# Loading the dense batches' expert weights once, into retired row buffers, with shorter packed rows

## The chip, the cores and the metric

The kernel runs on one core of a Trainium2 chip. The core has TensorE (PE, with its weight loads PEld), VectorE (DVE), ScalarE (ACT), GpSimd (POOL) and SyncE (SP); SP, ACT and POOL issue DMAs, which 16 DMA engines carry out. The metric is the device time of one execution in microseconds (us); of several runs the median is taken.

## What is computed

The input `x` has 64 batches of 256 rows of 256 float32 values. Two layers follow each other, each with attention over a graph and then a feed-forward part:

```
x = x + gnn0(layernorm(x), adj)              # 4 heads of 64, ELU at the end
x = x + (layernorm(x) @ weight.T + bias)
x = x + gnn1(layernorm(x), adj)              # 1 head of 256, ReLU at the end
x = x + moe(layernorm(x))
# gnn: q = h @ W; e = leaky_relu(q.a_src + q.a_dst), masked by adj; softmax(e) @ q
# moe: tokens t (16384 of them); probs = softmax(t @ router.T); the 2 best of 8 experts,
#      their weights made to sum to 1:
#      out = t + sum over the two e of weight_e * (gelu(t @ w1[e] + b1[e]) @ w2[e] + b2[e])
```

All of it is in float32. Which two experts a row goes to is known only on the chip.

## The kernel before

**Stages.** A generator `batch_layers` takes one batch through both attention layers, the feed-forward layer and the last norm. It leaves the normed rows in a tile `xe` of the ring tagged `xng`, which has `XNG` = 8 buffers of 128 partitions x 2 rows x 260 values (256 of the row and 4 of routing data). The mixture of experts is done in one of two ways:

- *Routed*, batches 0 to 60. `route` works in chunks of 4, 2 or 1 batches. It works out where each row goes and sends rows with indirect DMAs on POOL (`send`, L1066) from `xe` to a DRAM buffer `xs`, which is sorted by expert. `expert_pair` then works on 256 rows of one expert. On SP it loads the rows (`xr`, four DMAs at L906, in a ring of 5 buffers), their routing data (`xt`, L917, 14 buffers) and the expert's first weights (`we`, L935, a ring of `WBUFS` = 7 buffers). The rows are transposed on DVE (L117), `hidden` multiplies by the first weights (L968) and applies GELU (L974), `result` multiplies by the second weights (L983) and adds the bias (L993), ACT scales by the row's weight (L961). `scatter` (L1004) then adds the 256 rows to the output with two indirect DMAs on POOL. There are 129 pairs; the last 14 (`FLUSH`) are filled up with spare rows that are written at L1170.
- *Dense*, batches 61 to 63. `dense_expert` applies every expert to all rows of a batch and adds the result, weighted, to a tile `base` (L1036), which `store_dense` (L1047) stores at the end on SP. The batches are in two groups, {61} and {62, 63}; for each group each of the 8 experts is one job. Each of these 16 jobs loads the expert's first weights itself (L1026), into the same `we` ring that the routed pairs use. Second weights and biases (`w2s`, `b2s`) stay in SBUF for the whole kernel.

**Packed weights.** `pack_expert` writes each expert's first weights and bias into a DRAM tile `wpack[e]` of 128 rows of `WROW` values: 512 weights, from `C_B1` = 512 on two bias values, then zeros. `WROW` is 576 before, so a row has 2304 bytes.

**Order of the work.** The loop at the end writes the order out by hand, in steps, three (`TICKS`) for each new batch. Each job is a generator. What it yields is its rank in the next step (or, if negative, a rank in the same step); within a step jobs go on in the order of rank. The instructions of each engine, and of each DMA queue, run in the order thus written. In the step in which the job of expert 0 for batch 61 issues its load (at rank 90), batch 63 makes its `xe` tile (at rank 29); in the steps after it, one dense load and the loads of one pair follow each other on SP until all eight experts of the first group are loaded. `dense_free` spaces the jobs of the second group two steps apart.

**Waits.** A tile taken from a ring waits until all that used the buffer's last holder is done. A scatter waits until the two scatters of the pair before have landed (`added[-2:]`, L1001).

Of the kernel before, what the change touches and what calls it, by code (L numbers as in the profile page):

```python
# [9 lines left out]
F32 = mybir.dt.float32  # L10
# [5 lines left out]
P = 128  # L16
# [11 lines left out]
def kernel(  # L28
# [17 lines left out]
    nc = tc.nc  # L46
    B, N, D = x.shape
# [3 lines left out]
    KT = D // P  # L51
    NT = N // P
# [16 lines left out]
    ROW = D + 4  # L69
# [3 lines left out]
    io = ctx.enter_context(tc.tile_pool(name="io", bufs=2))  # L73
    work = ctx.enter_context(tc.tile_pool(name="work", bufs=2))
    small = ctx.enter_context(tc.tile_pool(name="small", bufs=4))
    keep = ctx.enter_context(tc.tile_pool(name="keep", bufs=1))
# [194 lines left out]

    C_B1, WROW = KT * D, KT * D + 64
    WBUFS, XBUFS, YBUFS = 7, 5, 9
    wpack = tc.dram_tile([E, P, WROW], F32, name="wpack")
    w2s = const.tile([P, E, KT * D], F32, tag="w2s", name="w2s")
# [41 lines left out]
    def once(work):  # L319
# [14 lines left out]
        out=tri, in_=tri, pattern=[[1, P]], base=0, channel_multiplier=-1,  # L334
# [157 lines left out]
    for i in range(2):  # L492
        t = keep.tile([P, NT, D + 1], F32, tag=f"q1_{i}", name=f"q1_{i}")
# [260 lines left out]
            dense_batch[b] = dict(base=base, xT=xT)  # L754

    XNG = 8
    dense_batch = {}

    def dense_home(b):

# [203 lines left out]
    def hidden(xT, we):  # L964
        ph = bank("ph", [KT, PAIR])
        for f in range(KT):
            for k in range(KT):
                nc.tensor.matmul(  # L968
                    ph[:, f, :], we[:, k * D + f * P : k * D + (f + 1) * P], xT[:, k, :],
                    start=(k == 0), stop=(k == KT - 1),  # L970
                )
        hT = work.tile([P, KT, PAIR], F32, tag="hT", name="hT", bufs=5)
        for f in range(KT):
            nc.scalar.activation(  # L974
                hT[:, f, :], ph[:, f, :], AF.Gelu, bias=we[:, C_B1 + f : C_B1 + f + 1]
            )
        return hT

    def product(hT, e):
        py = bank("py", [2, D])  # L980
        for t in range(2):
            for f in range(KT):
                nc.tensor.matmul(  # L983
                    py[:, t, :], hT[:, f, t * P : (t + 1) * P],
                    w2s[:, e, f * D : (f + 1) * D].rearrange("p e c -> p (e c)"),
                    start=(f == 0), stop=(f == KT - 1),
                )
        return py
# [33 lines left out]
    def dense_expert(e, group):  # L1022

        yield 90
        we = io.tile([P, WROW], F32, tag="we", name="we", bufs=WBUFS)
        nc.sync.dma_start(out=we, in_=wpack[e])  # L1026
        yield 40
        for b in group:
            own = dense_batch[b]
            yield 35  # L1030
            hT = hidden(own["xT"], we)
            yield -85
            py = product(hT, slice(e, e + 1))
            for t in range(NT):
                for add in (py[:, t, :], b2s[:, e, :]):
                    nc.vector.scalar_tensor_tensor(  # L1036
                        own["base"][:, t, :], add, own["w"][:, t, e : e + 1],
                        own["base"][:, t, :], op0=ALU.mult, op1=ALU.add,
                    )
            if e == E - 1:  # L1040
                begin(store_dense(b), 99)

    def store_dense(b):

        own = dense_batch[b]
        yield 99
        d = nc.sync.dma_start(  # L1047
            out=out_rows[b * N : (b + 1) * N, :].rearrange("(t p) d -> p t d", p=P),
            in_=own["base"],
        )  # L1050
        tc.declare_no_dep(d.ins, query=SYNC, group="out", reason="no row is added to here")
        tc.add_to_no_dep_group("out", d.ins)
        nc.sync.nop()
# [6 lines left out]
    def begin(job, rank):  # L1060
        active.append([rank, len(order), job])
        order.append(job)
# [126 lines left out]
    def route_dense(b, lg):  # L1189

        c = len(CHUNKS) + 1 + b - ROUTED
        ohs, ed = in_one(top_two(c, NT, lg, chunk_tile([NT], "first", c)))
        yield 75
        two = chunk_tile([2, NT], "two", c)
        nc.scalar.activation(two[:, 0], ed, AF.Tanh, scale=-0.5)
        second_weight(two[:, 1], two[:, 0])
        nc.vector.tensor_tensor(two[:, 0], two[:, 0], two[:, 1], ALU.add)
        w = chunk_tile([NT, E], "wd", c, DENSE)
        nc.vector.tensor_tensor(
            ohs, ohs, two[:, :, :, None].to_broadcast([P, 2, NT, E]), ALU.mult  # L1200
        )
        nc.vector.tensor_tensor(w, ohs[:, 0], ohs[:, 1], ALU.add)
        dense_batch[b]["w"] = w
        for group in GROUPS:
            if b == group[-1]:
                dense_jobs.extend(
                    (len(group), lambda e=e, g=group: dense_expert(e, g)) for e in range(E)
                )
# [109 lines left out]
```

## Time and profile before

| | |
|---|---|
| median of 3 runs | 1486.39 us (1485.40 to 1491.55) |
| profiled execution, its own time | 1489.83 us |
| its span, first to last instruction | 1488.0 us |
| mean granted TensorE clock | 0.985 |
| TensorE busy | 1420.1 us, 95% |
| VectorE, ScalarE, GpSimd busy | 83%, 68%, 58% |
| loads of first weights | 145, of 288 KB each |
| loads of rows `xr` | 516, of 64 KB each |
| scatters | 258 |
| DMA traffic | 236.10 MB, mean 159 GB/s |

The profile page gives busy time by engine, then the span in 40 equal slices with the busy share of each in tenths, then the chain of work that ended last, and the groups of instructions. Timelines list instructions of one engine: start, duration, engine, line, operation, tiles; in brackets is the idle time before it and what ended that, as far as the trace shows it. A DMA that SP issues is shown with the time of its issue[...]. The records of single packets give their queue, size, start and duration. Lists of waits give the engine and line, what it waited for, the sum in us, how often, and the longest.

### The profile page before, as it was taken

Reading aid. Unit: us, or ns where it says so; the run is one execution under the profiler, and the core shown is the slowest. Engines: PE = TensorE matmul, PEld = TensorE weight load, DVE = VectorE, ACT = ScalarE, POOL = GpSimd, SP = SyncE. Lnnn points to the kernel's source line nnn. Section 1 sums busy time; section 2 is a strip of 40 time slices with the busy share of each in tenths; the row PEclk is TensorE's granted clock in tenths of the full one; section 3 lists DMA queues with packets and bytes.
Section 4 is the critical chain, followed back from the end, with each engine's and each line's share of the span. In section 5 each row is a group of like instructions: output and inputs, shape, how many; then the busy total and the mean of one; then the engine's idle time right before and its main releaser. Section 6 shows DMA issues by size and latency. Waiting matters only on the chain. (4 is left out here: it accounts for less than half of the span.)

```text
span 1488.0 us, 29865 instructions
## 1 busy us (share of the span) xinstructions
PE 1420.1 (95%) x8138; PEld 1264.0 (85%) x8138; DVE 1232.9 (83%) x4320; ACT 1006.5 (68%) x2389; POOL 864.6 (58%) x851
## 2 busy tenths in 40 slices
PE   6899999999999999999999999999999999899994
PEld 5688888898999999899999989888888888778883
DVE  7689999988898889899888989998888888765442
ACT  1377667577777777777777787777777878643330
POOL 2122446455857676666758585776666668544444
PEclk9899999999999999999999999999999999999998
DMA  4832243567878777787877687768877786988743
GB/s 128 227 98 86 89 130 117 146 172 153 199 171 193 161 177 170 171 185 180 190 156 190 147 193 168 190 164 186 193 158 172 153 173 128 213 201 150 152 66 49
DMA packets 354081, 236.10 MB, mean 159 GB/s; under 512 B 246260, under 2 KB 316156, under 8 KB 353916
## 3 DMA queue, kind: packets, MB, share of 16 engines
q1 hardware_dynamic: 301000, 157.90, 42.1%
q0 software_dynamic: 48864, 66.33, 23.9%
q10 hardware_dynamic: 4052, 9.98, 2.3%
q8 instruction: 67, 1.10, 0.3%
q14 instruction: 98, 0.80, 0.2%
HBM read 146.00 MB, written 88.09 MB: 157 GB/s over the span
## 5 line engine op out<-in xcount | busy, mean ns | idle before, releaser
L1004 POOL DMA_INDIRECT out_dram<-y,xt x258 | 415.6, 1611 | 214.6 <-issue 54.6
L584 PE MATMUL pv<-q,z 128*128 128x65 f32 (+1 forms) x2560 | 363.7, 297 | 0.7 <-DVE z L570 0.3
L584 PEld LDWEIGHTS pv<-q,z 128*128 128x128 f32 x2560 | 331.2, 193 | 13.3 <-DVE z L570 1.3
L1066 POOL DMA_INDIRECT xs<-xng,pos x244 | 256.3, 1050 | 65.2 <-issue 57.7
L983 PE MATMUL py<-w2s,hT 128*128 (+1 forms) x1224 | 282.9, 382 | 4.7 <-ACT hT L974 4.5
L983 PEld LDWEIGHTS py<-w2s,hT 128*128 128x128 f32 x1224 | 229.7, 191 | 37.2 <-ACT hT L974 7.4
L570 DVE SCALAR_TENSOR_TENSOR z<-z,q,mask 128x256 f32<-128x256 f32 x504 | 231.5, 482 | 15.5 <-DMA z<-terms 6.5
L968 PE MATMUL ph<-sT,we 128*128 128x256 f32 x1032 | 241.4, 383 | 1.6 <-DVE sT L117 0.9
L968 PEld LDWEIGHTS ph<-sT,we 128*128 128x128 f32 x1032 | 195.6, 192 | 28.7 <-DVE sT L117 1.4
L961 ACT ACTIVATE y<-y,w 128x256 f32<-128x256 f32 x258 | 113.4, 499 | 119.4 <-DVE y L993 119.2
L459 ACT COPY xT<-pt 128x512 f32<-128x512 f32 x209 | 121.2, 588 | 82.1 <-PE pt L453 80.0
L974 ACT ACTIVATE hT<-ph,we 128x256 f32<-128x256 f32 x306 | 124.1, 472 | 64.1 <-PE ph L968 46.7
L406 POOL TENSOR_SCALAR rstd<-mv 128x4 f32<-128x4 f32 (+1 forms) x66 | 15.9, 240 | 224.8 <-DVE mv L379 175.3
L504 PE MATMUL pq<-wx,xT 128*128 128x259 f32 x512 | 126.5, 390 | 13.9 <-ACT xT L459 13.9
L424 ACT ACTIVATE off<-x,sums 128x256 f32<-128x256 f32 x256 | 129.2, 505 | 9.2 <-DVE x L667 3.3
L993 DVE TENSOR_TENSOR y<-py,b2s 128x512 f32<-128x512 f32 x129 | 86.9, 687 | 56.3 <-PE py L983 44.8
L469 PE MATMUL pq<-wx,xT 128*128 128x268 f32 x512 | 128.1, 394 | 2.4 <-DVE xT L117 1.2
L504 PEld LDWEIGHTS pq<-wx,xT 128*128 128x128 f32 x512 | 96.0, 192 | 33.6 <-ACT xT L459 19.8
L660 PE MATMUL pf<-wfT,xT 128*128 128x256 f32 x512 | 124.2, 386 | 0.0
L469 PEld LDWEIGHTS pq<-wx,xT 128*128 128x128 f32 x512 | 97.9, 192 | 21.7 <-DVE xT L117 1.4
L688 ACT ACTIVATE rel<-pv,rinv 128x256 f32<-128x256 f32 x128 | 54.0, 469 | 82.1 <-DVE rinv L591 81.8
L660 PEld LDWEIGHTS pf<-wfT,xT 128*128 128x128 f32 x512 | 94.9, 196 | 10.6
(170 smaller groups left out, 2355.7 us busy)
## 6 DMA issues: line engine op xcount, KB each, us to landing
we<-wpack SPq DMA_DIRECT2D x145, 288.0 KB
xr<-xs SPq DMA_DIRECT2D x516, 64.0 KB
z<-terms SPq DMA_DIRECT2D x46, 512.0 KB
xin<-in_x_dram SPq DMA_DIRECT2D x64, 256.0 KB
out_dram<-base SPq DMA_DIRECT2D x61, 256.0 KB
xblk<-in_x_dram SPq DMA_DIRECT2D x188, 64.0 KB
z<-terms ACTq DMA_DIRECT2D x17, 512.0 KB
out_dram<-y,xt POOLq DMA_INDIRECT x258
```

Source lines behind the costliest of these rows:

```text
L424: nc.scalar.activation(off, src[:, t, :], AF.Square, bias=sums[:, t : t + 1], scale=-float(D), accum_out=sq[:, at + t : at + t + 1],)
L459: nc.scalar.copy(dst, pt)
L469: nc.tensor.matmul(pq.rearrange("p h c -> p (h c)"), xT[:, k, t * P : (t + 1) * P], wx[:, k, :], start=(k == 0), stop=(k == KT - 1),)
L504: nc.tensor.matmul(pq, xT[:, k, t * P : (t + 1) * P], wx1[:, k, :], start=(k == 0), stop=(k == KT - 1),)
L570: nc.vector.scalar_tensor_tensor(z[:, j, :, h, :], terms, q[:, j, h, HD + 2 : HD + 3], masks[0][:, j, :].rearrange("p (t i) -> p t i", t=N ...
L584: nc.tensor.matmul(pv[:, h, :], z(j, h, t), q[:, j, h, : d + 1], start=(j == 0), stop=(j == NT - 1),)
L660: nc.tensor.matmul(pf[:, t, :], xT[:, k, t * P : (t + 1) * P], wfT[:, k, :], start=(k == 0), stop=(k == KT - 1),)
L968: nc.tensor.matmul(ph[:, f, :], we[:, k * D + f * P : k * D + (f + 1) * P], xT[:, k, :], start=(k == 0), stop=(k == KT - 1),)
L974: nc.scalar.activation(hT[:, f, :], ph[:, f, :], AF.Gelu, bias=we[:, C_B1 + f : C_B1 + f + 1])
L983: nc.tensor.matmul(py[:, t, :], hT[:, f, t * P : (t + 1) * P], w2s[:, e, f * D : (f + 1) * D].rearrange("p e c -> p (e c)"), start=(f == 0 ...
L1004: d = nc.gpsimd.indirect_dma_start(out=out_rows, out_offset=bass.IndirectOffsetOnAxis(ap=xt[:, t, 0:1].bitcast(I32), axis=0), in_=y[:, t, ...
L1066: d = nc.gpsimd.indirect_dma_start(out=xs_d[: E * CAP * PAIR, :], out_offset=bass.IndirectOffsetOnAxis(ap=at, axis=0), in_=xe, in_offset=None,
```

## The change

- A packed row has 512 + 16 values, 2112 bytes, rather than 2304. This holds for the packing, and for the routed pairs' loads.
- A dense job loads its expert's first weights only if no dense job has loaded them before. The tile comes from the ring `xng` of normed rows rather than from `we`, and holds 514 values (2056 bytes) in each partition. The tiles are kept in a dictionary `dense_weights`, so the second group's jobs find the first group's.

No other instruction is added, removed or moved in the written order.

```
-    C_B1, WROW = KT * D, KT * D + 64
+    C_B1, WROW = KT * D, KT * D + 16
...
-    dense_batch = {}
+    dense_batch, dense_weights = {}, {}
...
     def dense_expert(e, group):
 
         yield 90
-        we = io.tile([P, WROW], F32, tag="we", name="we", bufs=WBUFS)
-        nc.sync.dma_start(out=we, in_=wpack[e])
+        if e not in dense_weights:
+            we = keep.tile([P, NT, ROW], F32, tag="xng", name=f"wd_{e}", bufs=XNG)
+            we = we.rearrange("p t c -> p (t c)")[:, : C_B1 + KT]
+            nc.sync.dma_start(out=we, in_=wpack[e, :, : C_B1 + KT])
+            dense_weights[e] = we
+        we = dense_weights[e]
         yield 40
         for b in group:
             own = dense_batch[b]
```

## The prediction, made before the changed kernel had run

> **What bounds the kernel now.** I read the page first for the balance of the engines, then the chain that ended last in order of time, then the timelines of POOL and SP over the last 180 us, where the change acts. The page says that one engine is nearly full:
>
> ```profile
> span 1488.0 us, 29865 instructions
> PE 1420.1 (95%) x8138; PEld 1264.0 (85%) x8138; DVE 1232.9 (83%) x4320; ACT 1006.5 (68%) x2389; POOL 864.6 (58%) x851
> PE   6899999999999999999999999999999999899994
> DMA  4832243567878777787877687768877786988743
> ```
>
> From slice 2 to slice 39 TensorE is at 80% or more, nearly always at 90%; the DMA engines are at 60 to 90%. In most of the span a transfer that comes sooner gains nothing. The end is different. The chain in order of time, its last 55 us:
>
> ```profile
> 1432.13 3.45 PE py L983 x16
> 1435.58 3.47 PE ph L968 x16
> 1439.22 0.28 issue
> 1439.51 0.48 ACT hT L974
> 1440.01 3.77 DMA out_dram<-y,xt
> 1443.91 0.71 issue
> 1444.62 1.56 POOL out_dram L1004
> ...
> 1478.34 1.56 POOL out_dram L1004
> 1479.89 1.86 POOLq L1313
> ```
>
> The last thing to end is not TensorE (its last matmul starts at 1467.28) but the scatters of L1004: two per pair of 256 rows, and each pair's scatter waits until the one before has landed. The chain view hands over to TensorE at 1439, but the trace shows that this is not where the scatters begin to set the pace. The last pair's rows `y` are weighted at 1447.67 and scattered from 1478.34, 31 us later; a pair at 1347 is already 25 us behind its `y`, and from 1317 on none is under 15 us. So over the whole tail the scatters run one behind the other. POOL's timeline gives the time of a step (first scatter of a pair to the first of the next):
>
> ```profile
> 1309.86 1.61 POOL L1004 DMA_INDIRECT out_dram<-y,xt  x1 [1.55 <-DMA out_dram<-y,xt]
> ...
> 1346.98 1.56 POOL L1004 DMA_INDIRECT out_dram<-y,xt  x1 [4.04 <-DMA xr<-xs]
> ...
> 1355.23 1.56 POOL L1004 DMA_INDIRECT out_dram<-y,xt  x1 [4.83 <-DMA xr<-xs]
> ...
> 1406.30 1.56 POOL L1004 DMA_INDIRECT out_dram<-y,xt  x1 [4.00 <-DMA xr<-xs]
> ...
> 1464.02 1.56 POOL L1004 DMA_INDIRECT out_dram<-y,xt  x1 [3.04 <-ACT hT L974]
> ```
>
> From 1406.30 to 1464.02 there are 9 steps: 6.41 us each. From 1309.86 to 1406.30 there are 13: 7.42 us each, 8.25 in the worst (1346.98 to 1355.23). The 13 steps are 96.44 - 13 x 6.41 = 13.1 us longer than undisturbed ones. These 13.1 us are all that the change can reach on the path that sets the end. By the packet records of those steps: the packets of a scattered pair take 3.0 to 3.2 us where nothing else moves; beside weights and rows they take up to 4.7. Over the 25 last steps this window is fitted, within 0.11 us, by 3.09 + 0.62 x (engine time of weight packets inside it) + 0.35 x (of rows `xr` and `xt`) + 0.58 x (of a store). The weights have 11.8 us inside the 13 windows, so 7.3 us of the 13.1; rows 9.3 us, so 3.3; one store 0.4; the remaining 2.1 is a later start of five of the windows.
>
> **Part 1: eight loads less.** SP's timeline, and what SP waited for in this tail:
>
> ```profile
> 1341.52 0.35 SPq L935 DMA_DIRECT2D we<-wpack  x1
> 1343.30 0.35 SPq L1026 DMA_DIRECT2D we<-wpack  x1
> 1343.88 1.94 SPq L906 DMA_DIRECT2D xr<-xs  x4
> ...
> SPq L1026 <- PE ph L968: 28.1, 12, 5.7
> ```
>
> L1026 is a dense load, L935 a routed one. Sixteen dense loads become eight: those of the second group (issued at 1357.11, 1369.14, 1382.96, 1396.77 and four from 1410.58 to 1424.40) go. The last four lie behind 1406.30, where their packets (from 1.0 to 2.5 us after issue) miss the scatter windows: no gain. Between 1309.86 and 1406.30 there are 27 weight loads (16 routed, 11 dense); 4 go. Taking the 7.3 us as spread evenly, 23/27 of it stays, 6.2 us: a gain of 1.1. The bounds: 0.3 us, because by their time of issue only the one of 1357.11 overlaps a window (0.85 us of weights in that step, at most half of it this load's, x 0.62), and 3.0 us, from comparing the six steps with one pair and one dense load each (1.15 us above 6.41) with the later seven that have fewer dense loads (0.88); solved for two unknowns, this gives 0.34 a pair and 0.75 a dense load, which hangs on the phases. I take 1.1.
>
> Here a rule bears. The Trainium skill ("DMA: Bandwidth & Descriptors", section "Queues, rings and completion order") says that a DMA engine takes turns between the queues that have work, a packet at a time. By it a microsecond of weights in a window would cost up to a whole microsecond, 11.8 in place of 7.3, and part 1 would give 1.7. The fit to the windows says 0.62; I use the fit.
>
> **Part 2: rows of 2112 bytes.** A routed load keeps its 128 packets, each 2112 bytes instead of 2304; a dense one has 2056. In the records a packet of 2304 bytes takes 93 ns in the median and one of 2080 bytes 85 ns, so 2112 should take 86: a load's engine time goes from 128 x 93/16 = 744 to 688 ns. A page speaks against this edit: by the skill (same page, section "How a descriptor splits into AXI transactions") reads go in 32-byte beats from 256-byte boundaries, and bytes ahead of an unaligned start are fetched too. 2304 is nine times 256, so with an aligned start every row is 72 beats; 2112 leaves three rows of four off the boundary, 69 beats on average rather than 66, hence 89 ns instead of 86. The row of 2080-byte packets is nearer, though these are stores into the row buffer and not reads from it; the two differ by 24 ns a load. On 6.2 us it gives 8% (by the rule 4%): 0.5 us (0.25). In the rest of the kernel it saves some 115 x 56 ns = 6.4 us of engine time, hidden under a TensorE that is over 95% busy and that gets its weights many microseconds ahead: nothing. Should that cover go, it would be 56 ns a pair at most.
>
> **Part 3: the new place of the dense weights, and its wait.** Ring order: batch 63's rows are made in the scheduler step in which the first dense load is issued, and ahead of it (rank 29 against 90). So the eight loads take the buffers of batches 56 to 63 in turn. What each waits for: for batches 56 to 59, sends issued by 1285.6; for 60, the send of 1307.32; for 61 to 63, transposes on TensorE, the last at 1314.04, and POOL's iota for batch 63 at 1320.32. The load that takes 60's buffer is issued at 1329.48 now and can't go before about 1327, behind the first flushed pair's rows at 1321.09; those on 61 to 63 come behind it. Every buffer is free by then: no wait, cost nothing. Behind these loads on SP stand the routed loads of the flushed pairs and then the dense stores. If a wait arose here, a pair's rows would come later; the one lead the trace shows well is rows at 1350.80 for a transpose at 1368.82, 18 us.
>
> **Part 4: the wait that goes, and what is late next.** Of the waits for a free `we` buffer, L1026 has 28.1 + 9.6 us and L935 8.3 in the tail. They hide behind TensorE now, which runs from 1315.29 to 1442.33 without a gap (a routed and a dense expert take 4 x 1.727 = 6.91 us): no gain there. But SP runs ahead. The next limit is the ring of five `xr`: a pair's rows can be asked for when the pair five earlier has been transposed. That brings rows of 1336.97 to about 1332.6, of 1357.69 to 1344, of 1371.86 to 1355.5. Then SP stands at the store of batch 61, which needs DVE's addition of 1374.89, and goes on with the last four pairs from 1376 to 1393, 8 to 11 us sooner than now. The scatters meet the same routed loads in fewer steps: those of 1324 to 1345 are worse (about 8.1 us), the one of 1362 and those after 1393 are free. Laying the issue times on the steps with the fit, all four parts together come to -2.0 us; without the shift I had -1.6. From both sides: -4 if the bursts fall between windows, +3 if they fall into them.
>
> **Sum.** -1.1 - 0.5 - 0.4 = -2.0 us. The span becomes 1486.0; the profiled execution's 1489.83, which includes 1.8 outside the span, becomes 1487.8. It lies 3.4 above the median of the runs, within their spread, so I take the 2.0 from the median: 1484.4 us.
>
> **Rivals.** (a) The loads removed lay beside the windows anyway, and the same routed bytes disturb the same chain: 1486.4. For it: only one of the four is seen in a window. Against: smaller packets still help. (b) The chain is freed: if the earlier rows slip between the windows, and weights and rows cost half, 1.6 + 0.5 x (13.1 - 1.6) = 7.4 us go, down to 1479; more is barred, since the dense stores (issued up to 1471) and the 3.2 us of ending put a floor near 1478 in the span. Against: 16 routed loads remain. (c) **Slower**: the freed SP, released by transposes every 6.91 us, bunches its loads ahead, and its bursts fall in step with the scatters, which disturbed take about the same time. Its place is the scatters of 1310 to 1400. Each such step would be like the worst, 8.25 us: 13 x (8.25 - 7.42) = 10.8 us more, 1497. It is slower by over 0.5% from a mean of 7.99 on. Against: a scatter that takes 8.25 falls out of step with 6.91 at once. (d) The change doesn't take effect: the removed loads are certain, so only as (a).
>
> **How the numbers follow.** Chances: the forecast 0.52 (1481 to 1487), (a) 0.20 (1484 to 1490), (b) 0.14 (1474 to 1479), (c) 0.14 (1494 to 1500). A measurement of this kernel can tell about 0.5%, 7.4 us, from no change: faster is below 1479.0, slower above 1493.8. So faster 0.14, same 0.72, slower 0.14. The range 1477 to 1495 cuts some half of (b) and most of (c), under 2 in 10.
>
> **What would show it.** 137 weight loads, eight of them of the dense kind, all before 1350. No wait of L1026 on TensorE or ScalarE; SP's rows reach the store of batch 61 some 15 us sooner. TensorE without a gap in the tail, still 6.91 us a pair. Scatter steps of 6.4 us from about 1395 rather than 1406; the sum of the 13 steps around 94.4. Wrong would be: a gap on TensorE before a dense `ph`, an L1026 that waits for a send, a main part that is longer by microseconds up to 1310, or steps that are disturbed by more than 8 us on average.

## The result, and the profile after

| | before | after |
|---|---|---|
| median of 22 runs each, on one chip | 1489.35 us (1480.22 to 1497.85) | 1486.49 us (1482.45 to 1491.73) |
| ratio after / before, 95% interval | | 0.9973 [0.9961, 0.9986] |
| profiled execution, its own time | 1489.83 us | 1486.08 us |
| its span | 1488.0 us | 1484.3 us |
| mean granted TensorE clock | 0.985 | 0.985 |

By the ratio the changed kernel is faster by 0.27%: 4.0 us, from 2.1 to 5.8. The ratio, here and below, is an estimate from all the runs of both kernels; it is not the quotient of the two medians. Those differ by 2.9 us, 0.19%, which lies inside the interval. A second comparison gave 0.9976 [0.9962, 0.9990]. The gain is real and small. It is below the 0.5% that the prediction took as the least that counts as a change, so the case "same" holds. The forecast was -2.0 us.

The head of the page and two rows of the slices, after:

```profile
span 1484.3 us, 29844 instructions
PE 1418.8 (96%) x8138; PEld 1263.9 (85%) x8138; DVE 1232.3 (83%) x4320; ACT 1007.0 (68%) x2389; POOL 865.3 (58%) x851
PE   6899999999999999999999999999999999899994
DMA  4822334566878777777877777868878775987533
```

No engine has another amount of work, and TensorE's row is the same digit for digit. In the page's list of DMA issues, the routed loads now move 264 KB each instead of 288:

```profile
we<-wpack SPq DMA_DIRECT2D x129, 264.0 KB
```

The last steps of the chain that ended last, in order of time (start, duration, engine, tiles or line):

```profile
1463.12 0.50 DVE dbase L1040
1465.08 2.33 DMA out_dram<-dbase
1467.41 1.56 POOL out_dram L1004
1469.27 3.92 DMA out_dram<-y,xt
1474.73 1.56 POOL out_dram L1004
1476.29 1.86 POOLq L1317
```

The end has the same form as before: the last pair's two scatters, then the closing step. The last pair's first scatter starts at 1474.73 instead of 1478.34, 3.6 us sooner, which is the whole difference of the spans (3.7).

Did these 3.6 us arise in the tail, where the prediction had put them? POOL's timeline after has the first scatters of pairs:

```profile
1306.56 1.61 POOL L1004 DMA_INDIRECT out_dram<-y,xt  x1 [1.01 <-DMA out_dram<-y,xt]
...
1327.96 1.56 POOL L1004 DMA_INDIRECT out_dram<-y,xt  x1 [4.20 <-DMA xr<-xs]
...
1337.05 1.56 POOL L1004 DMA_INDIRECT out_dram<-y,xt  x1 [5.67 <-DMA xr<-xs]
...
1387.39 1.55 POOL L1004 DMA_INDIRECT out_dram<-y,xt  x1 [3.53 <-DMA out_dram<-y,xt]
...
1395.67 1.57 POOL L1004 DMA_INDIRECT out_dram<-y,xt  x1 [4.86 <-ACT hT L974]
...
1402.22 1.56 POOL L1004 DMA_INDIRECT out_dram<-y,xt  x1 [3.10 <-ACT hT L974]
...
1461.02 1.55 POOL L1004 DMA_INDIRECT out_dram<-y,xt  x1 [3.12 <-DMA out_dram<-y,xt]
```

In these two profiles they did not. The first pair of the tail scatters at 1306.56; before it was at 1309.86. So 3.3 of the 3.6 us were there when the tail began. The 13 steps from 1306.56 to 1402.22 take 95.7 us (before 96.4), the nine to 1461.02 take 58.8 (before 57.7). The lead can be followed back to the very start. ACT's timeline has one exponential at L645 for each batch; that of batch 5 is here, first before, then after:

```profile
100.44 0.63 ACT L645 ACTIVATE e<-hp 128x512 f32<-128x512 f32 x1
```

```profile
96.91 0.63 ACT L645 ACTIVATE e<-hp 128x512 f32<-128x512 f32 x1
```

It is 3.5 us sooner. Batch by batch the lead is 0.4 us at batch 0, 0.8 at batch 1, 3.2 at batch 2, 3.7 at batch 3, 3.5 at batch 5, 3.5 at batch 17. Up to batch 56 it stays between 3.1 and 3.6; in the tail the lead of single scatters swings between 1.9 and 5.0. Nearly all of it comes from 30 to 75 us, while the packing of the weights goes on.

One pair of profiles can mislead, and the second profile of the changed kernel shows by how much. There batch 5 begins at 97.0 and batch 63 is still 3.6 us ahead of the first profile of before. But its first scatter of the tail is at 1307.83, 2.0 us ahead, and the last pair's at 1477.74, 0.6 us ahead: the tail took back what the start had given.

SP's timeline in the tail, before and then after, and SP's waits there after:

```profile
1379.36 0.41 SPq L1047 DMA_DIRECT2D out_dram<-dbase  x1
...
1400.76 1.92 SPq L906 DMA_DIRECT2D xr<-xs  x4
```

```profile
1339.64 0.54 SPq L1028 DMA_DIRECT2D wd<-wpack  x1
...
1373.57 0.40 SPq L1051 DMA_DIRECT2D out_dram<-dbase  x1
...
1388.43 1.92 SPq L906 DMA_DIRECT2D xr<-xs  x4
```

```profile
SPq L1051 <- DVE dbase L1040: 77.2, 2, 73.4
SPq L1051 <- DVE w L951: 9.9, 1, 9.9
SPq L935 <- ACT hT L974: 0.8, 2, 0.4
```

L1028 is the dense load, eight in all, the last at 1339.64. It has no wait. SP reaches the store of batch 61 (L1051) at about 1364 and stands there for 9.9 us. Before, it was there at about 1379. So SP's schedule is as forecast, and the last pair's rows are asked for at 1388.43 instead of 1400.76. TensorE runs without a gap from 1311.8 to about 1448, at 6.91 us a pair as before. Yet the scatters did not get faster.

### The profile page after: what moved, and what is told of

It reads as the page before. It is cut to its first block, busy times and chain, and to the rows that moved or that the text cites. A ratio compares the mean times of both kernels' runs of the same rounds, so it can differ in the third digit from the quotient of the medians.

```text
span 1484.3 us, 29844 instructions
## 1 busy us (share of the span) xinstructions
PE 1418.8 (96%) x8138; PEld 1263.9 (85%) x8138; DVE 1232.3 (83%) x4320; ACT 1007.0 (68%) x2389; POOL 865.3 (58%) x851
## 5 line engine op out<-in xcount | busy, mean ns | idle before, releaser
L1004 POOL DMA_INDIRECT out_dram<-y,xt x258 | 416.6, 1615 | 212.1 <-issue 57.9
L570 DVE SCALAR_TENSOR_TENSOR z<-z,q,mask 128x256 f32<-128x256 f32 x504 | 231.6, 482 | 12.3 <-DMA z<-terms 3.3
L974 ACT ACTIVATE hT<-ph,we 128x256 f32<-128x256 f32 x258 | 104.1, 472 | 30.7 <-PE ph L968 26.3
L504 PEld LDWEIGHTS pq<-wx,xT 128*128 128x128 f32 x512 | 96.4, 192 | 30.9 <-ACT xT L459 17.0
```

The source lines that it names most:

```text
L504: nc.tensor.matmul(pq, xT[:, k, t * P : (t + 1) * P], wx1[:, k, :], start=(k == 0), stop=(k == KT - 1),)
L570: nc.vector.scalar_tensor_tensor(z[:, j, :, h, :], terms, q[:, j, h, HD + 2 : HD + 3], masks[0][:, j, :].rearrange("p (t i) -> p t i", t=N ...
L1004: d = nc.gpsimd.indirect_dma_start(out=out_rows, out_offset=bass.IndirectOffsetOnAxis(ap=xt[:, t, 0:1].bitcast(I32), axis=0), in_=y[:, t, ...
```

## The experiments

Each run had the kernel before beside it on the same chip, and each ratio is to that; the medians of a table needn't give the same quotient. The numbers in the stage tables come from one profiled execution per kernel. "Batch 5" is the start of its exponential. "13 steps" and "9 steps" are the scatter steps that the prediction sums. "Weights inside" is the engine time of weight packets inside the 13 scatter windows.

### Which part gives the gain

The short rows alone, in the kernel before:

```
-    C_B1, WROW = KT * D, KT * D + 64
+    C_B1, WROW = KT * D, KT * D + 16
```

> Only the shorter packed rows (2112 bytes), the dense loads as before. Theory A (the prediction): the gain lies in the tail, in the windows of the scatters; rows alone give -0.5 us, and the first batches keep their times. Theory B (read from the two profiles: all of the 3.5 us by which the changed kernel is ahead is there at batch 2, at 57 us, while the experts are packed): rows alone give -3 to -4 us, batch 2's exponential (L645) comes 3 us sooner, and the 25 last scatters take as long as before, 168.5 us. Theory C (chance of one execution): no shift of batch 2 that repeats, and a ratio that contains 1.

The sharing alone, in the kernel after:

```
-    C_B1, WROW = KT * D, KT * D + 16
+    C_B1, WROW = KT * D, KT * D + 64
```

> Only the sharing of the dense weights in the ring of normed rows, packed rows of 2304 bytes. Theory A: -1.5 us, all after 1300 us: the span from the first scatter of pair 104 to that of pair 128 falls from 168.5 to about 167. Theory B: batch 2 as before (57 us), and in the tail nothing to -0.5 us, so a ratio of 1.000 within 0.001. Theory C: 1.000.

Both on one chip, where the kernel before took 1487.26 us:

| kernel | median us | ratio | batch 5 | 13 steps | 9 steps | weights inside |
|---|---|---|---|---|---|---|
| before (first profile) | | | 100.4 | 96.4 | 57.7 | 11.8 |
| after (first profile) | | | 96.9 | 95.7 | 58.8 | 8.3 |
| short rows alone | 1485.12 | 0.9976 [0.9963, 0.9989] | 97.2 | 97.5 | 57.4 | 10.9 |
| sharing alone | 1486.43 | 1.0000 [0.9987, 1.0013] | 100.8 | 94.8 | 57.9 | 12.1 |

By the ratios the rows give 3.6 us of the 4.0 (1.6 to 5.5, from the interval times 1487). The sharing by itself shows 0.0, with 1.9 us either way. By the medians it is 2.1 us for the rows and 0.8 for the sharing. The sum agrees with the change either way, but the split is loose and has to be read with the clock, further below. The tail of the sharing alone took 166.4 us, near the 167 of theory A; but tails range from 162.4 to 170.5 us over all profiles, so one tail can't decide it. The start goes with the rows in these two profiles, from batch 3 on (70.1 us with the rows, 74.5 with the sharing; batch 2, where the shift was expected, stays at 56.7 with the rows). Batch 5 of the kernel with short rows, then of the one with sharing:

```profile
97.18 0.63 ACT L645 ACTIVATE e<-hp 128x512 f32<-128x512 f32 x1
```

```profile
100.83 0.63 ACT L645 ACTIVATE e<-hp 128x512 f32<-128x512 f32 x1
```

### Loads or packing

A row of 2112 bytes shortens three things: the routed loads, the writes of the packing, and the distance between rows in DRAM. In the first of these kernels only the loads are cut; packed rows keep 2304 bytes. This is the edit at L935, and L1026 is cut in the same way:

```
-            out=we, in_=wpack[bass.ds(e_sp, 1), :, :].rearrange("e p c -> (e p) c")
+            out=we[:, : C_B1 + 16],
+            in_=wpack[bass.ds(e_sp, 1), :, : C_B1 + 16].rearrange("e p c -> (e p) c"),
```

> The kernel before with packing as it was (rows of 2304 bytes written and kept 2304 apart) but all loads of first weights cut to 2112 bytes of each row. Theory A: -0.5 us, as for shorter rows. Theory B: nothing, since the packing at the start is untouched: batch 2 at 57 us as before, ratio 1.000 within 0.001. If it gains as much as shorter rows do, the packing isn't the cause.

The second also writes only 2112 bytes of each row; the rows still lie 2304 apart:

```
-        nc.vector.memset(wt[:, C_B1:], 0.0)
+        nc.vector.memset(wt[:, C_B1 : C_B1 + 16], 0.0)
...
-        nc.sync.dma_start(out=wpack[e], in_=wt)
+        nc.sync.dma_start(out=wpack[e, :, : C_B1 + 16], in_=wt[:, : C_B1 + 16])
```

> As the run with all loads cut to 2112 bytes and rows 2304 apart, and now the packing writes 2112 bytes a row too; dense loads not shared. It moves the same bytes as the shorter rows alone, but each row starts on a multiple of 256 bytes. Theory B (bytes of the packing): as the shorter rows alone, -3.5 us, batch 3 at 70 us. If the distance of the rows matters instead (the skill's rule on reads from 256-byte boundaries), faster than the shorter rows by up to 24 ns a load of 2112 bytes, under 1 us in all as far as it is not hidden. If the start's shift was chance: -1.5 us, as with the loads alone, and batch 3 at 73 to 75.

| kernel | median us | ratio | batch 5 |
|---|---|---|---|
| loads cut | 1485.09 | 0.9990 [0.9978, 1.0003] | 99.2 |
| loads and packing cut (another chip, before 1488.75) | 1487.12 | 0.9985 [0.9974, 0.9996] | 97.8 |
| change as given, again (same chip as the line above) | 1484.84 | 0.9976 [0.9962, 0.9990] | 97.0 |

> The changed kernel once more, on the chip of the runs beside it. Theory A (tail) and B (start) alike: ratio 0.997 to 0.998. B: batch 3's exponential (L645) at 70 to 71 us again, against 73 to 75 where experts are packed in rows of 2304 bytes. The 25 last scatters: A about 166.5 us, B 162 to 169 without a rule.

The three ratios fall in the order in which more is cut, but their intervals overlap, so none of the shares is separated. What the profiles do separate is the start: with packing writes of 2304 bytes batch 5 begins at 99.2 to 100.8 (three kernels), with 2112 at 96.9 to 97.8 (four). That speaks for the packing; what follows speaks less for it. The packets themselves leave nothing open: the median of a routed load's packet is 93 ns for 2304 bytes and 86 ns for 2112, whether the rows lie 2112 or 2304 bytes apart.

### Is it the bytes of the packing?

If it is, writing every packed row a second time, to a DRAM tile that nobody reads, should cost much more than the 192 bytes a row gain:

```
+    wspare = tc.dram_tile([E, P, WROW], F32, name="wspare")
...
         nc.sync.dma_start(out=wpack[e], in_=wt)
+        nc.sync.dma_start(out=wspare[e], in_=wt)
```

> The changed kernel, and each packed expert is written a second time, to a spare place in DRAM: 8 DMAs of 264 KB more while the start's DMA engines are full, 2.1 MB, at the 250 GB/s of that stretch 8.4 us of DMA time. Theory B (the start waits for its DMAs): batch 3 comes 4 to 9 us later than in the changed kernel (75 to 80 us), and the kernel is 4 to 9 us slower than it, 1.000 to 1.004 of the kernel before. Theory A and chance: the writes are hidden, within 1 us of the changed kernel.

1485.30 us, 0.9976 [0.9965, 0.9987]: the same as the change without it. Batch 5 begins at 99.2, 2.2 us later than in the change on the same chip. The second writes are 2.2 MB, eleven times what the short rows save (8 x 128 x 192 bytes = 0.2 MB). Bytes alone don't explain it then: at 2.2 us for 2.2 MB the 0.2 MB would be worth 0.2 us, and the start moved by 3. The row of windows from 40 to 78 us tells the same. Its columns are the stretch, its length, busy time and count of PE, PEld, DVE, ACT and POOL, the granted clock, the DMA engines' share and GB/s. Before, after, and with the packing written twice:

```profile
40.00:78.00 38.00, 33.09 (x164) 26.79 (x163) 25.07 (x80) 16.06 (x46) 5.21 (x10) 0.82 0.81 238
```

```profile
40.00:78.00 38.00, 33.31 (x178) 28.33 (x177) 28.17 (x87) 19.44 (x54) 6.37 (x10) 0.87 0.79 236
```

```profile
40.00:78.00 38.00, 33.68 (x171) 27.79 (x170) 26.38 (x85) 17.37 (x49) 6.41 (x10) 0.91 0.82 253
```

The DMA engines are at 80% in this stretch, and full for parts of it, as a shorter stretch of before shows:

```profile
40.00:45.00 5.00, 2.22 (x10) 1.58 (x9) 1.63 (x3) 2.68 (x7) 0.99 (x2) 0.53 1.00 284
```

So a transfer can matter here: PE gets through 178 matmul instructions after and 164 before. But the granted clock differs as well. It can't be the whole reason, since the kernel with sharing alone has 0.87 as after and the late start of before. The clock records of the traces say how much it can be: the clock is at half for stretches of 3.4 us or a multiple, which ahead of batch 5 come to 13.7 us before and 10.2 after. The difference of 3.4 us at half clock is worth at most 1.7 of the 3.5 us. In the second profile of the kernel before, further below, it is 10.2 us as well, and its start is not late. How much of the lead is bytes, clock or order of issue is not settled.

Then the packing alone was undone in the change: rows of 2304 bytes again, with only the loads at L935 cut to 528 values by the edit shown above.

> The changed kernel with the packing alone undone: rows of 2304 bytes are filled, written and kept; every load still takes 2112 or 2056 bytes, dense weights shared. Start theory: the kernels with rows of 2304 bytes reach batch 5's exponential (L645) at 99.2 to 100.8 us, those with 2112 at 96.9 to 97.8; so here about 100, and a ratio of 0.999 to 1.000. Loads or tail as the cause: batch 5 at 97, and 0.9975. If writing twice as much at the start (2.1 MB) cost 2.2 us at batch 5, bytes alone (0.2 MB) explain 0.2 us, and a full 3 us here would mean that the length of the rows, not the sum of bytes, counts.

It ran on a third chip, beside a run of the kernel before against itself:

> The kernel before against itself: ratio 1.000 within the interval. Its profile is a second look at the start and the tail: start theory says batch 5 at 99 to 101 us; the 25 last scatters at 162 to 170 us, as all kernels have shown whatever their loads.

On this chip the kernel before takes 1509.4 us. The packing undone gave 0.9993 [0.9973, 1.0013], the kernel before against itself 1.0011 [0.9992, 1.0031]. Batch 5 begins at 98.7 and at 97.8. The estimate for 2304-byte packing lies where the theory of the packing puts it, near no gain, but its interval reaches to 0.9973, and on this chip the start of the kernel before is not late. The change with less work for TensorE (the last experiment), which packs short rows, begins batch 5 on this chip at 97.4, only 0.4 us sooner than the kernel before. The lead at the start is there in the first two profiles and among the kernels of the first chip of the experiments; that the packing is its cause is not shown.

### The same runs at equal clock

Each run has its mean granted clock, and the runs of one kernel differ by it. In 143 runs of the kernel before, on the two chips of the experiments so far (the third left out), the time falls by 9.7 us for each 0.01 of clock (correlation -0.72). The kernels' mean clocks differ from it by up to 0.0017, each +- 0.0007 to 0.0013. The mean time less that of the kernel before on the same chip, as measured and with 9.7 us per 0.01 taken off for the difference of the clocks:

| kernel | clock less before's | mean time less before's, us | at equal clock, us |
|---|---|---|---|
| short rows alone | +0.0011 | -2.8 | -1.8 +- 1.0 |
| sharing alone | -0.0008 | -0.7 | -1.4 +- 1.0 |
| loads cut | 0.0000 | -2.7 | -2.7 +- 1.2 |
| loads and packing cut | +0.0009 | -2.4 | -1.6 +- 1.3 |
| change as given, again | +0.0008 | -3.3 | -2.5 +- 0.9 |
| packing written twice | +0.0017 | -3.1 | -1.4 +- 0.8 |

The +- are two standard errors. Part of what the clock costs can be seen in single stretches. Of the profiles that are not from the third chip, three have no stretch at half clock near 290 us (short rows alone, sharing alone, loads cut); they take 733.9 us from batch 5 to batch 45. All others have one of 6.8 us there, and take 735.7 to 735.8. Read thus, the sharing does give something, 0.4 to 2.4 us, and the rows less than their ratio says, 0.8 to 2.8. The loads with the packing left as it was give as much as the loads with it cut, so the packing is no needed part of the gain. The second writing costs about 1 us against the change, within the errors. The correction has a limit: it treats the clock as chance and as the cause of the time, which a correlation can't show. Where a kernel changes the clock itself, it misleads: in the kernel with less work for TensorE (the last experiment) the clock is 0.55 in the 25 us after its last matmul, and its mean falls to 0.977 with no time lost. So the correction weakens the split by ratios and doesn't replace it.

### A start that is earlier by other means

With rows of 2056 bytes there is no padding and the memset at L282 is not needed:

```
-    C_B1, WROW = KT * D, KT * D + 16
+    C_B1, WROW = KT * D, KT * D + KT
...
-        nc.vector.memset(wt[:, C_B1:], 0.0)
```

> The changed kernel with rows of 2056 bytes (512 weights, 2 biases, no pad), and so without VectorE's filling of the pad (L282). SP's third DMA for an expert (the bias, L287) waits for that filling now, from 14.6 to 33.8 us, while the DMA engines are at 1% of their time; after that they are full until 60 us. Theory A: as the changed kernel, -2 us against before, since only 56 bytes a row go. Theory B: without the wait the packing starts at 15 us in the idle stretch, the DMA engines are less than full from 40 to 60 us, the terms of batches 1 and 2 land sooner, and batch 2 comes another 3 to 8 us sooner than in the changed kernel: -6 to -12 us against before. If only bytes count and not when they move, -1 us on top of the changed kernel.

The next kernel has the same values, in rows that lie 2304 bytes apart in DRAM:

```
-    wpack = tc.dram_tile([E, P, WROW], F32, name="wpack")
+    wpack = tc.dram_tile([E, P, KT * D + 64], F32, name="wpack")
...
-        nc.sync.dma_start(out=wpack[e], in_=wt)
+        nc.sync.dma_start(out=wpack[e, :, :WROW], in_=wt)
```

The loads at L935 read the same columns.

> No pad and no filling, 514 columns moved (2056 bytes), but rows kept 2304 bytes apart in DRAM; dense weights shared. Theory B: as the run without a pad, batch 3 at 67 us, -4.5 us against before. With a gain from rows on 256-byte boundaries: up to 1 us more. Theory A: -2 us.

| kernel | median us | ratio | batch 3 | batch 5 | 13 steps | weights inside |
|---|---|---|---|---|---|---|
| no padding | 1482.70 | 0.9970 [0.9959, 0.9982] | 67.1 | 95.5 | 92.3 | 5.7 |
| no padding, rows 2304 apart | 1484.61 | 0.9970 [0.9957, 0.9982] | 65.8 | 92.6 | 94.6 | 10.3 |

Both are 4.5 us below the kernel before by the ratio, less than the 6 to 12 us that the theory of the start gave; at equal clock, as in the table above, they are 4.0 +- 0.9 and 3.4 +- 1.0 us below. The distance of the rows in DRAM shows no difference between their ratios. These are the best ratios of the study, but the ratio of the change, 0.9973 or 0.9976, lies inside their intervals. What the memset did is plain on SP's timeline. Before, then without padding:

```profile
14.00 0.47 SPq L283 DMA_DIRECT2D wt<-in_L_ffn_w_dram  x1
34.19 0.37 SPq L287 DMA_DIRECT2D wt<-in_L_ffn_b_dram  x1
```

```profile
14.02 0.47 SPq L282 DMA_DIRECT2D wt<-in_L_ffn_w_dram  x1
14.53 0.43 SPq L286 DMA_DIRECT2D wt<-in_L_ffn_b_dram  x1
...
27.35 0.40 SPq L295 DMA_DIRECT2D wpack<-wt  x1
```

The bias load follows the memset into the same tile. The memset stands in DVE's order behind the first batches' statistics, so SP stands for 19.9 us, and with it everything that SP has to issue. SP's waits before have it (sum, times, longest):

```profile
SPq L287 <- DVE stats L378: 23.2, 3, 19.9
```

Without it the first packed write goes at 27.35 instead of about 36.

### Do loads in the tail matter, and what sets the end?

To put loads back into the tail, each of the 16 dense jobs of the kernel without padding loads 1792 bytes a row into a tile that nobody uses:

```
+        dead = io.tile([P, 448], F32, tag="dead", name=f"dead_{e}", bufs=1)
+        nc.sync.dma_start(out=dead, in_=wpack[e, :, :448])
```

> The kernel without a pad (2056 bytes a row), and each of the 16 dense jobs loads 448 columns of its weights (1792 bytes a row) once more into a buffer that nobody reads: 16 loads more in the tail where the change took 8 away. By the prediction's fit, about half of the loads issued before 1406 us fall into a window of the scatters, at 0.62: 12 x 0.58 us x 0.5 x 0.62 = 2.2 us, so about 0.9985 against the 0.997 of the same kernel without them, and the steps of the scatters before 1406 us are longer by about 2 us in all. If the tail doesn't feel weight loads: 0.997.

1511.14 us on the third chip, 1.0021 [1.0003, 1.0039]; the tail from the first scatter of pair 104 to that of the last pair is 170.5 us. The same kernel without the dead loads had 0.9970 and 163.9 us, but on another chip, and here the kernel before against itself came to 1.0011 and has a tail of 170.0. Inside the 13 scatter windows are 11.6 us of weight packets with the dead loads and 5.7 without, and the 13 steps take 98.2 us and 92.3. This fits loads that cost time in the tail, more than the 2.2 us expected, and doesn't prove it: the two kernels were not side by side.

The last experiment takes work from TensorE. Experts 4, 5 and 6 are left out for batches 62 and 63; no load and no scatter is touched:

```
             yield 35
+            if len(group) == 2 and 3 < e < E - 1:
+                continue
```

> The changed kernel, experts 4, 5 and 6 left out for batches 62 and 63 (their sums are then incomplete): 6 times 3.45 us of TensorE less in the tail, 20.7 us. If the scatters set the end, the span falls by less than 3 us (their chain and its loads are untouched; the rows come a little sooner). If TensorE sets the end, as the chain view has it up to 1439 us, it falls by 10 us or more.

1505.45 us, 0.9988 [0.9968, 1.0008]. Twelve blocks of 1.727 us are gone, 20.7 us in all, and the time didn't follow. TensorE's last matmuls, the last pair's first scatter, and the chain that ended last:

```profile
1460.11 1.99 PE L983 MATMUL py<-w2s,hT 128*128 128x256 f32 x8 [0.63 <-ACT hT L974]
```

```profile
1492.86 1.56 POOL L1004 DMA_INDIRECT out_dram<-y,xt  x1 [3.82 <-issue]
```

```profile
1468.14 3.77 DMA out_dram<-y,xt
...
1481.06 3.72 DMA out_dram<-y,xt
...
1487.48 3.83 DMA out_dram<-y,xt
```

The last matmul ends at 1462.1; in the kernel before on the same chip it is at 1491.4. The last pair's first scatter is at 1492.9 against 1501.0, of which 6.4 us were there when the tail began. The tail takes 168.3 us against 170.0. So the scatters set the end in both, as the prediction said. This also shows how the chain of waits is to be read. With TensorE's end 30 us before the last scatter, the chain names the scatters for the last 50 us; in the kernels with all the work it hands over to TensorE at about 1440 or in the last steps, because the last releaser changes, though the scatters have been behind since 1310.

## Why the prediction was right, and where it was off

**What bounds the kernel: right.** The scatters' chain sets the end. Leaving out 20.7 us of TensorE's work in the tail moved the time by 0.12% (interval -0.32% to +0.08%), so not measurably.

**Part 1, eight loads less, -1.1: not refuted, not seen without the clock.** The loads went, 137 remain, and the dense ones all go before 1350. The weights inside the 13 windows fell from 11.8 to 8.3 us in the first profile after and to 9.7 in the repeat (11.4 in a second profile before). At 0.62 that is 1.3 to 2.2 us of gain. The 13 steps became shorter by 0.7, 96.4 to 95.7, and in the second profiles, on two chips, 97.5 and 97.0. The sharing alone, which has parts 1, 3 and 4 in it and -1.5 by the prediction, measured 0.00% +- 0.13% as a ratio, and -1.4 +- 1.0 us at equal clock. So the size fits, but only with that correction. What the profiles show is why it is small against the noise. Over the 13 profiles for which weights inside were summed, these range from 5.4 to 12.1 us and the 13 steps from 89.3 to 97.5, with a correlation of 0.73 and a slope of 0.70 us per us. The mechanism stands: a window with more of these packets in it is longer. The price is known roughly: a fit of the prediction's form gives 0.79 in the first profile after and 0.44 in the second, with about twice the scatter of the one before. How much of the same loads falls inside a window is set by the phases: the kernel before with its loads cut has 5.4, the one with short rows has 10.9, with the same number of loads of the same size. Taking the weights "as spread evenly" gives a mean of something that varies more than the change moves it.

**Part 2, shorter rows, -0.5: too small as far as can be told, and with a term left out.** Measured alone, 3.6 us (1.6 to 5.5) by the ratio, 2.1 by the medians and 1.8 (0.8 to 2.8) at equal clock. The same bytes in rows 2304 apart gave 1.6 +- 1.3 at equal clock, which still holds 0.5. The packet's price was exact, 86 ns; the rule of the Trainium skill ("DMA: Bandwidth & Descriptors", "How a descriptor splits into AXI transactions") weighed against it would have made 89 by the prediction's estimate and is not visible here, with rows 2112 or 2304 bytes apart. The sentence that doesn't hold as it stands is that the rest of the kernel saves "nothing". It counted the routed loads only, and covered them with a TensorE at 95%. The packing's eight writes were not counted at all, although the text on the change names them, and they lie at the start, where the cover doesn't hold: the page's slices of before have DMA at 8 in the second slice with PE at 8, and the windows there show the DMA engines at 81% over 38 us. There the lead of 3.5 us arose in the first pair of profiles, and in that pair it came through to the end: from batch 5 to batch 17 takes 177.6 us in both, and from there to the first scatter of the tail 1031.9 and 1032.1. Whether the short rows made it is not settled. The second profile of the kernel before begins batch 5 at 97.8, so 2.7 of the 3.5 us also lie between two executions of one kernel, on two chips. What the short rows give, and where, stays open too: the loads alone gave 1.5 us by the ratio and 2.7 at equal clock, with the late start left as it was, and the bytes of the packing alone would give 0.2. So the sum of a start that is 3 us sooner and of smaller loads is not what any one run shows.

**Part 3, no wait at the new place, 0: right.** L1028 has no wait in the profile after.

**Part 4, SP runs ahead, -0.4: the schedule right, the gain not seen.** The store of batch 61 was reached 15 us sooner, as forecast, and the last pair's rows went 12.3 us sooner, of which 3.5 is the earlier start. The steps early in the tail did get worse, as forecast (7.6, 9.1, 8.1 and 7.9 us up to 1353, where about 8.1 was named). The undisturbed steps begin at 1395.67, with 6.55, as forecast, against 1406 before; but the step just ahead of it, which was to be free, took 8.28. The 13 steps together took 95.7 us and not the 94.4 of the forecast: the worse steps used up most of what the earlier end gained.

**The rivals.** (a), nothing reaches the chain, fits the tail in the profiles, 168.5 and 170.0 us before, 168.2 and 169.9 after; it was wrong on the total, which did fall. (b), the chain freed, didn't come: the 13 steps are still 95.7 - 13 x 6.53 = 10.8 us longer than the later ones. (c), bunching, didn't come either: the mean step is 7.36 us and 7.99 was its point.

**How much of it was luck.** The sign held and the time lies in the range. But the range of 1477 to 1495 holds the kernel before as well, so a change of nothing would have hit it too. The forecast of 1484.4 was counted from a median of three runs, 1486.39; the 22 runs have 1489.35. And in the first pair of profiles the place was wrong for nine tenths of the gain (3.3 of 3.7 us of the span): the tail, in which the prediction had put all of it, can't be told from chance. That the size, -2.0 against 2.9 by the medians and 4.0 by the ratio, came out near is in good part luck.

## What to carry to other kernels

List every place that a changed constant reaches, and cost each with the bound of its own stage: here the start, with its DMA engines at 81%, was left out of the sum, and in the profiles it moved by 3 us. Where work can be followed by item (an exponential per batch, a scatter per pair), compare the same item's time in both traces first: it shows in which stage a gain arose. Then look at a second profile of each kernel before calling it the cause: here starts of one kernel lay 2.7 us apart, and tails over all kernels 8. To test whether an engine sets the end, take work from it: if the end stays, it was not that engine, whatever the chain of waits names.

## What the runs showed of the hardware

- **Run to run, half of the variance goes with the clock.** With 9.7 us per 0.01 taken out, the standard deviation of the 143 runs falls from 2.9 to 2.0 us. A change of 2 us is as large as 0.002 of clock, which is also the standard deviation of the clock from run to run. In the traces the lower clock is a few stretches of 3.4 or 6.8 us at half clock; one of 6.8 us near 290 us went with 1.9 us.
- **Chips differ at nearly the same clock.** The kernel before took 1487.26 and 1488.75 us on two chips and 1509.4 on a third, with mean clocks of 0.986, 0.985 and 0.984. The profile puts the difference into the steady part: from batch 17 to the first scatter of the tail it took 1055.6 us there and 1031.9 in the first profile, start and tail alike. Ratios are comparable between the chips, times are not.
- **Packets.** 2304 bytes took 93 ns, 2112 bytes 86, 2056 to 2080 bytes 85. The distance of the rows in DRAM played no part.
